# Router and feed-forward part of a sandwich layer: float32r halves replaced by fp16 halves scaled by powers of two

## The chip, the cores and the metric

One NeuronCore of a Trainium2 chip runs the whole program. The metric is the device time of one execution in microseconds (us); three runs of the kernel before are known, and one further execution was profiled.

## The reference, cut to what matters

```python
x = x + ln(attention(ln(x)))     # 2048 tokens of 256, 16 heads of 128
x = x + ln(ffn(ln(x)))

def ffn(x):                      # 8 experts, inner width 176, top 2
    probs = softmax(x @ Wr)      # router, [256, 8]
    w, i  = top_k(probs, 2);  w = w / sum(w)
    g = einsum('bsh,ehi->besi', x, Wg)
    u = einsum('bsh,ehi->besi', x, Wu)
    y = einsum('besi,eih->besh', silu(g) * u, Wd)
    return sum over e of combine[e] * y[e]
```

Weights, inputs and result are float32. The attention weights come as fp4 codes with block scales. `ln` is a layer norm without gain and bias, so it gives the same result for any power of two that multiplies its input, if its epsilon is multiplied by the square of that power.

## The kernel before, in words

The kernel reaches float32 accuracy by splitting each operand into a high and a low half and doing three products: high by high, high by low, low by high. In attention both halves are fp16 (HP); in the router and the feed-forward part both halves are float32r. Everything is recorded under a manual schedule, so the order of instructions on each engine is the order of the Python calls, and each engine works through its own list in order.

**Attention** is a loop of 258 steps `g` (L676), 16 heads of 16 query tiles (`h, t = divmod(g, 16)`). A step does on TensorE twelve 512-column matmuls of scores (`scores_half`, L447, two halves of six) and twelve of probabilities times values (`pv_unit`, L517 to L519, two units of six) for tiles further back. VectorE takes the maxima of both halves (L458), the negated maximum (L462), the inverse of the sum (L476, L479) and the low half of the probabilities (`pl`, L498, two pieces). ScalarE does two exponentials (L469) and the high half (`ph`, L483). SP then transposes `ph` and `pl` by DMA (L486, L502) into `pt`. Scores are in three PSUM buffers, `pl` in two of SBUF, `ph` in three.

`fill(h, t)` (L538) adds projections for later heads to a step: a query or key projection (four matmuls of 512 columns, L191) in even `t`, a value projection (four of 256, L216) in odd `t` of an odd head. Its PSUM tile has the tag `pj`, of which there is one; ScalarE copies it out (L204, L235) after the exponentials of that step, and GpSimd splits it. In even heads `load_w` brings the next head pair's codes and scales through GpSimd's DMA queue (L130, L135) at `t` = 0, 3 and 6, 512 KB each time. Every fourth step GpSimd writes 256 KB of attention output to memory (`ot_d`, L533).

**The last head** (`late`, L647) also loads the rest of the output weights and the gate weights `wg`, and splits these in four pieces (`split_piece`, L602: a high copy on ScalarE, a subtraction on GpSimd). The up weights `uw` and down weights `dw` are split after attention, before the feed-forward loop.

**The router** transposes a normed block of 512 tokens (`tr`, L808), splits it, and multiplies it by `rw` (L833); its logits go through a top-2 on VectorE, and the combine weights through memory (`ct_d`), from where they are broadcast as `cu`.

**The feed-forward loop** (L1112) has four blocks of 512 tokens by eleven chunks of 128 inner columns, 44 chunks in all. `gate_up` (L906) does 12 matmuls of 512 columns (L914); ScalarE takes the sigmoid (L934), VectorE three products (L935, L936, L939), ScalarE the high half of the hidden value and GpSimd its low half (L927, L928). `down` (L943), two chunks behind, does 12 matmuls of 256 columns (L953). Between the chunks lie the output projection of later blocks (L759, fp16 by bf16), the norms on VectorE, and the router of the next block.

Of the kernel before, what the change touches and what calls it, by code (L numbers as in the profile page):

```python
# [8 lines left out]
F32 = mybir.dt.float32  # L9
# [21 lines left out]
ISQ = 1.0 / 128.0 ** 0.5  # L31
XS = 1024.0
PS = 16384.0
POOL_COLS = 512


@with_exitstack
def sandwich(
# [35 lines left out]
    ssc = const.tile([128, 2], F32)  # L74
    sgv = const.tile([128, 1], F32)

    def rstd_of(mv, n, pool):
        v = pool.tile([128, n], F32, name="ln_v")
        nc.vector.tensor_scalar(v, mv[:, :, 1], EPS, None, ALU.add)
# [7 lines left out]
    one3 = const.tile([3, 128], F32)  # L87
    bvT = bT[:, 2]
    bv3 = const.tile([128, NH, 3], BF)
    crow = const.tile([128, D], F32)  # L90
    rst = const.tile([128, 2, E], F32)
    rw = const.tile([128, 2, 2, E], F32R)
    res = const.tile([128, 2, NH], F32)

    def tail_consts(i):
        if i == 0:
            nc.sync.dma_start(out=crow, in_=bo.partition_broadcast(128))
            nc.sync.dma_start(out=rst, in_=wr.rearrange("(kc p) e -> p kc e", p=128))
            nc.gpsimd.iota(iota8, [[1, 8]], base=0, channel_multiplier=0,
                           allow_small_or_imprecise_dtypes=True)  # L100
        else:
            nc.gpsimd.tensor_copy(bv3[:, :, 0], bvT)
            nc.gpsimd.tensor_tensor(res[:, 0], bvT, bv3[:, :, 0], ALU.subtract)
            nc.gpsimd.tensor_copy(bv3[:, :, 1], res[:, 0])
            nc.gpsimd.tensor_tensor(res[:, 1], res[:, 0], bv3[:, :, 1], ALU.subtract)
            nc.gpsimd.tensor_copy(bv3[:, :, 2], res[:, 1])
            nc.gpsimd.tensor_copy(rw[:, 0], rst)
            nc.gpsimd.tensor_tensor(rw[:, 1], rst, rw[:, 0].bitcast(F32), ALU.subtract)

    small = ctx.enter_context(tc.tile_pool(name="small", bufs=4))  # L110
    proj_ctx = ExitStack()
# [127 lines left out]
    with tc.tile_pool(name="start", bufs=4) as st:  # L239
# [18 lines left out]
        for i, (which, codes, scales) in enumerate(  # L258
# [8 lines left out]
        nc.gpsimd.memset(one3, 1.0)  # L267

        make_identity(nc, ident)
        def scale_bcast(which, ps):  # L270
# [32 lines left out]
        def sig_pow():  # L303
            nc.vector.tensor_reduce(t3[:, 0:1], sgp["t"][:3, :128], AX.X, ALU.max)
            nc.vector.tensor_scalar(t3[:, 1:2], t3[:, 0:1], 1e-30, None, ALU.max)
            nc.vector.tensor_scalar(
                t3.bitcast(I32)[:, 2:3], t3.bitcast(I32)[:, 1:2], 0x7F800000, None,
                ALU.bitwise_and,
            )
            nc.vector.tensor_scalar(t3[:, 3:6], ident[:3, :3], t3[:, 2:3], None, ALU.mult)  # L310
            ps = psA.tile([128, 512], F32, name="sgb", tag="pj")
            nc.tensor.matmul(ps[:, :3], one3, t3[:, 3:6], start=True, stop=True)
            sgp["s"] = ps

        def sig_all():
# [280 lines left out]

    def bias_row2(b3):
        pb2 = psA.tile([128, 512], F32, name="pb2", tag="pj")
        nc.tensor.matmul(pb2[:, :D], one3, b3, start=True, stop=True)
        nc.vector.tensor_tensor(crow, pb2[:, :D], crow, ALU.add)  # L600

    def split_piece(dst, stg, on_pool):  # L602
        nc.scalar.copy(dst[0], stg)
        eng = nc.gpsimd if on_pool else nc.vector
        eng.tensor_tensor(dst[1], stg, dst[0].bitcast(F32), ALU.subtract)

    gu_raw = {}

# [6 lines left out]
        )  # L615
        return stg

    def split_gu(dst, i, stg, on_pool):
        kc, eh = divmod(i, 2)
        cs = slice(4 * I * eh, 4 * I * eh + 4 * I)  # L620
        split_piece(
            (dst[:, 0, kc, cs], dst[:, 1, kc, cs]),
            stg.rearrange("p e i -> p (e i)"), on_pool,
        )

    OIN = {}
# [20 lines left out]
    def late(t):  # L647
        nonlocal gw
        if t in WO_LOAD:
            load_wo(3 + WO_LOAD.index(t), kqv, ("kT", "kT"), 8)  # L650
        if t - 1 in WO_LOAD:
            dequant_wo(3 + WO_LOAD.index(t - 1))
        if t == 13:
            bias_row2(gst.pop("b3"))
        if t == 12:
            gst["b3"] = bias_row()
        if t == 9:
            proj_ctx.close()
            rp = ctx.enter_context(tc.tile_pool(name="gw", bufs=1, side="right"))
            gw = rp.tile([128, 2, 2, EI], F32R)  # L660
        if 10 <= t < 14:
            split_gu(gw, t - 10, gst.pop(t - 10), True)
# [13 lines left out]
    for g in range(NS + 2):  # L676
# [123 lines left out]
    def ln_b2(b):  # L800
        MV2[b] = small.tile([128, 4, 2], F32, name="mv2")
        stats(X1[b], MV2[b], 0, 4)
        R2[b] = rstd_of(MV2[b], 4, small)

    def ln_c(b):
        norm(AT[b], X1[b], MV2[b], R2[b])

    def tr(b, kc, tag="pj"):  # L808
        xn = AT[b]
        if kc == 0 and b == 0:  # L810
            XT[b] = [
                kqv.tile([128, 2, 512], F32R, name="xT0", tag="v", bufs=7)
                for _ in range(2)
            ]
        elif kc == 0:
            xt = tl.tile([128, 2, 2, 512], F32R, name="xT", bufs=2)
            XT[b] = [xt[:, 0], xt[:, 1]]
        xh, xl = XT[b]
        ps = aux_psum([128, 512], F32, "trp", tag)
        for t in range(4):  # L820
            nc.tensor.transpose(ps[:, bass.ts(t, 128)], xn[:, t, bass.ts(kc, 128)], ident)
        nc.scalar.copy(xh[:, kc], ps)
        nc.vector.tensor_tensor(xl[:, kc], ps, xh[:, kc].bitcast(F32), ALU.subtract)

    LGT, LG, CW = {}, {}, {}

    def router_a(b, tag="pj"):
        xT = XT[b]
        ps = aux_psum([8, 512], F32, "rp", tag)
        n = 0  # L830
        for kc in range(2):
            for a, w in ((0, 0), (1, 0), (0, 1)):
                nc.tensor.matmul(  # L833
                    ps, rw[:, w, kc, :], xT[a][:, kc, :], start=(n == 0), stop=(n == 5)
                )
# [43 lines left out]
    def router_d(b):  # L879
        cw = CW.pop(b)  # L880
        pc = psA.tile([E, 512], F32, name="pct", tag="pj")
        for t in range(4):
            nc.tensor.transpose(pc[:, bass.ts(t, 128)], cw[:, 0, t, :], ident)
        ct = small.tile([E, 512], F32, name="cT", bufs=1)
        nc.scalar.copy(ct, pc)
        nc.sync.dma_start(out=ct_d[b], in_=ct)

    CU = {}
# [17 lines left out]
    def gate_up(b, c):  # L906
# [11 lines left out]
                    n += 1  # L918
        sg = tl.tile([128, 512], F32, name="sg", bufs=3)
        cu = CU.pop((b, c))  # L920
        hh = tl.tile([128, 2, 512], F32R, name="hh", bufs=3)
        ends = b == 3 and c >= NCH - 2
        parts = 2 if b == 3 and c == NCH - 1 else 1

        def low(f):
            fs = bass.ts(f, 512 // parts)
            nc.scalar.copy(hh[:, 0, fs], sg[:, fs])  # L927
            (nc.vector if ends else nc.gpsimd).tensor_tensor(  # L928
                hh[:, 1, fs], sg[:, fs], hh[:, 0, fs].bitcast(F32), ALU.subtract
            )  # L930

        for f in range(parts):
            fs = bass.ts(f, 512 // parts)
            nc.scalar.activation(sg[:, fs], ps[:, 0, fs], AF.Sigmoid)  # L934
# [33 lines left out]
    def fin1(b):  # L968
        MV3[b] = small.tile([128, 4, 2], F32, name="mv3")
        stats(YT[b], MV3[b], 0, 4)  # L970
        R3[b] = rstd_of(MV3[b], 4, small)

    def fin2(b):
        y = YT[b]
# [10 lines left out]
    def fin_last(b):  # L985
# [189 lines left out]
```

## Time and profile before

| What | us |
|---|---|
| median of three runs | 1884.12 (1881.57 to 1884.13) |
| the profiled execution, its own time | 1879.05 |
| its span, first to last instruction | 1877.3 |
| attention loop, first to last score maximum (L458) | 31.3 to 1582.0 |
| an odd head without weight loads (1, 3, 5, 7, 9, 11, 13), each | 94.3 |
| even heads 2, 4, 6, 8, 10, 12 | 98.1, 97.7, 99.7, 99.0, 97.1, 100.8 |
| first feed-forward chunk to the last (L914) | about 1641 to 1865 |

A head is taken from the L462 of its first step to that of the next head. The profile lists, by line, engine and operation, how often an instruction ran and how long one took. The mean duration of a TensorE matmul is longer than the distance between two starts, since consecutive ones overlap; for matmuls the distance of starts in the timeline is the cost. "Idle before" names what ended the waiting of an engine.

### The profile page before, as it was taken

Reading aid. Unit: us, or ns where it says so; the run is one execution under the profiler, and the core shown is the slowest. Engines: PE = TensorE matmul, PEld = TensorE weight load, DVE = VectorE, ACT = ScalarE, POOL = GpSimd, SP = SyncE. Lnnn points to the kernel's source line nnn. Section 1 sums busy time; section 2 is a strip of 40 time slices with the busy share of each in tenths; the row PEclk is TensorE's granted clock in tenths of the full one; section 3 lists DMA queues with packets and bytes.
Section 4 is the critical chain, followed back from the end, with each engine's and each line's share of the span. In section 5 each row is a group of like instructions: output and inputs, shape, how many; then the busy total and the mean of one; then the engine's idle time right before and its main releaser. Section 6 shows DMA issues by size and latency. Waiting matters only on the chain. (4 is left out here: it accounts for less than half of the span.)

```text
span 1877.3 us, 25533 instructions
## 1 busy us (share of the span) xinstructions
PE 1794.1 (96%) x8890; PEld 936.0 (50%) x8890; DVE 1632.4 (87%) x2267; ACT 1365.5 (73%) x1730; POOL 907.5 (48%) x893
## 2 busy tenths in 40 slices
PE   7899999999999999999999999999999988899998
PEld 4344444444444444444444444444444434588887
DVE  7999989998999899998999999889999886458566
ACT  5888878888888788887888888778888776123232
POOL 3554574457544654465445644564444342233222
PEclk9999999999999999999999999999999999999999
DMA  3999999999999999999999999999999999982121
GB/s 91 190 193 190 189 202 198 190 189 202 196 191 189 193 195 191 192 201 193 188 190 205 197 189 192 183 202 194 191 186 205 208 220 219 259 236 69 55 71 57
DMA packets 1133345, 342.31 MB, mean 182 GB/s; under 512 B 1070896, under 2 KB 1120768, under 8 KB 1133216
## 3 DMA queue, kind: packets, MB, share of 16 engines
q1 hardware_dynamic: 1120528, 310.53, 90.4%
q0 software_dynamic: 9584, 27.82, 5.9%
q10 hardware_dynamic: 3104, 2.33, 0.5%
q8 instruction: 70, 1.15, 0.2%
q14 instruction: 59, 0.48, 0.1%
HBM read 53.22 MB, written 18.94 MB: 38 GB/s over the span
## 5 line engine op out<-in xcount | busy, mean ns | idle before, releaser
L498 DVE SCALAR_TENSOR_TENSOR pl<-p,m,ph 128x1024 f16<-128x1024 f32 x512 | 731.6, 1429 | 50.2 <-DMA pt<-pl 43.9
L469 ACT ACTIVATE p<-s,m,ssc 128x1024 f32<-128x1024 f32 x512 | 611.9, 1199 | 192.6 <-DVE m L462 158.9
L458 DVE TENSOR_REDUCE m<-s 128x1 f32<-128x1024 f32 x512 | 622.0, 1215 | 23.2 <-PE s L457 22.7
L483 ACT ACTIVATE ph<-p,m 128x2048 f16<-128x2048 f32 x256 | 513.0, 2004 | 84.7 <-issue 30.2
L518 PE MATMUL pv<-pt,v 128*128 128x512 f16 x1024 | 391.2, 382 | 27.9 <-DMA pt<-pl 27.9
L453 PE MATMUL s<-kT,qT 128*128 128x512 f16 x1024 | 389.9, 381 | 16.9 <-ACT p L469 13.9
L517 PE MATMUL pv<-pt,v 128*128 128x512 f16 x1024 | 390.6, 381 | 7.4 <-DMA pt<-ph 5.3
L519 PE MATMUL pv<-pt,v 128*128 128x512 f16 x1024 | 391.2, 382 | 0.0
L454 PE MATMUL s<-kT,qT 128*128 128x512 f16 x1024 | 389.8, 381 | 0.0
L457 PE MATMUL s<-kT,qT 128*128 128x512 f16 x1024 | 305.3, 380 | 0.0
L205 POOL CAST qT<-t 128x512 f16<-128x512 f32 x63 | 86.4, 1371 | 247.2 <-ACT t L204 247.2
L236 POOL CAST v<-t 128x256 f16<-128x256 f32 (+1 forms) x105 | 54.3, 517 | 271.8 <-ACT t L235 271.8
L518 PEld LDWEIGHTS <-v 128*128 128x128 f16 x1024 | 100.7, 98 | 153.8 <-issue 29.4
L454 PEld LDWEIGHTS <-qT 128*128 128x128 f16 x1024 | 100.4, 98 | 135.2 <-issue 33.4
L517 PEld LDWEIGHTS <-v 128*128 128x128 f16 x1024 | 100.6, 98 | 130.8 <-issue 7.0
L519 PEld LDWEIGHTS <-v 128*128 128x128 f16 x1024 | 100.7, 98 | 123.6 <-issue 7.6
L457 PEld LDWEIGHTS <-qT 128*128 128x128 f16 x1024 | 100.5, 98 | 121.8 <-issue 1.7
L453 PEld LDWEIGHTS <-qT 128*128 128x128 f16 x1024 | 100.6, 98 | 111.3 <-issue 3.2
L237 POOL TENSOR_TENSOR v<-t,v 128x256 f16<-128x256 f32 (+1 forms) x105 | 146.8, 1398 | 8.4
L928 POOL TENSOR_TENSOR hh<-sg,hh 128x512 fp32r<-128x512 f32 x42 | 54.5, 1298 | 144.6 <-ACT hh L927 99.4
L927 ACT CAST hh<-sg 128x512 fp32r<-128x512 f32 (+1 forms) x45 | 27.5, 611 | 118.4 <-DVE sg L939 118.4
L206 POOL TENSOR_TENSOR kT<-t,kT 128x512 f16<-128x512 f32 x60 | 107.8, 1796 | 5.0
(184 smaller groups left out, 2019.4 us busy)
## 6 DMA issues: line engine op xcount, KB each, us to landing
oi<-ot_d SPq DMA_DIRECT2D x32, 512.0 KB, 6.9
ot_d<-o POOLq DMA_DIRECT2D x63, 256.0 KB, 4.1
pt<-ph SPq DMA_TRANSPOSE x256, 5.1
pt<-pl SPq DMA_TRANSPOSE x256, 4.7
cu<-ct_d SPq DMA_DIRECT2D x16, 256.0 KB, 3.9
xt<-in_L_attn_x SPq DMA_DIRECT2D x4, 512.0 KB, 5.6
wos<-in_L_attn_wo_scales ACTq DMA_DIRECT2D x32, 64.0 KB, 4.5
woc<-in_L_attn_wo_codes SPq DMA_DIRECT2D x8, 256.0 KB, 3.5
```

The costliest lines, as they stand in the source:

```text
L206: nc.gpsimd.tensor_tensor(t[:, 1, :], t32, t[:, 0, :], ALU.subtract)
L237: nc.gpsimd.tensor_tensor(v[:, 1, sl, :], t32, v[:, 0, sl, :], ALU.subtract)
L453: nc.tensor.matmul(s[:, j, :], q[:, 0, qc], k[:, 0, :], start=True, stop=False)
L454: nc.tensor.matmul(s[:, j, :], q[:, 0, qc], k[:, 1, :], start=False, stop=False)
L457: nc.tensor.matmul(s[:, j, :], q[:, 1, qc], k[:, 0, :], start=False, stop=True)
L458: nc.vector.tensor_reduce(m[:, half : half + 1], s, AX.XY, ALU.max)
L469: nc.scalar.activation(p[:, bass.ts(i, 1024)], s, AF.Exp, bias=m[:, 2:3], scale=ssc[:, 0:1], accum_out=m[:, 3 + i : 4 + i],)
L483: nc.scalar.activation(ph, p, AF.Copy, scale=m[:, 6:7])
L498: nc.vector.scalar_tensor_tensor(pl[:, cs], p[:, cs], m[:, 6:7], ph[:, cs], ALU.mult, ALU.subtract)
L517: nc.tensor.matmul(ps, vh, d[:, :, c, :], start=(c == 0), stop=False)
L518: nc.tensor.matmul(ps, vh, d[:, :, 16 + c, :], start=False, stop=False)
L519: nc.tensor.matmul(ps, vl, d[:, :, c, :], start=False, stop=(c == 15))
```

## The change

Router and feed-forward operands (`rw`, the normed input `xT`, `gw`, `uw`, `dw`, the hidden value `hh`) become pairs of fp16 in place of float32r. To keep fp16 in range, each weight is multiplied by 1024 divided by the power of two of its largest entry. These four maxima are found by the kernel:

- `max_load` and `max_piece`: the three expert weights (1.44 MB each) are read a second time, in 24 pieces of 128x352 (180 KB) through GpSimd's DMA queue, one every second step of heads 3, 4 and 5; VectorE reduces each piece three steps later, in odd `t`, with one further small reduction after every eighth.
- `wscale`: in head 7, after steps 3, 5 and 7, three stages bring the maxima across partitions (a TensorE transpose, a small matmul that broadcasts, 15 small VectorE instructions) and split `rw`.
- `split_piece` gets one more ScalarE pass over each of the eleven staged weight pieces; the subtraction stays on GpSimd.
- The sigmoid, the logits' copy and the combine weights' copy take a scale in the ScalarE instruction that they had; the norms take a scaled epsilon.

```diff
-    rw = const.tile([128, 2, 2, E], F32R)
+    rw = const.tile([128, 2, 2, E], HP)
...
-            nc.gpsimd.tensor_copy(rw[:, 0], rst)
-            nc.gpsimd.tensor_tensor(rw[:, 1], rst, rw[:, 0].bitcast(F32), ALU.subtract)
+    def max_load(i, j):
+        src = (wg, wu, wd)[i].rearrange("e a b -> (e a b)").rearrange("(p n) -> p n", p=128)
+        wms[(i, j)] = stage.tile([128, 352], F32, name="wmx", bufs=2)
+        nc.gpsimd.dma_start(out=wms[(i, j)], in_=src[:, bass.ts(j, 352)])
+    def max_piece(i, j):
+        if j == 0:
+            wms[i] = small.tile([128, 8], F32, name="wms", bufs=1)
+        nc.vector.tensor_reduce(
+            wms[i][:, j : j + 1], wms.pop((i, j)), AX.X, ALU.max,
+            apply_absolute_value=True,
+        )
+        if j == 7:
+            nc.vector.tensor_reduce(wm[:, i : i + 1], wms.pop(i), AX.X, ALU.max)
+    def wscale(i):
+        if i == 0:
+            nc.vector.tensor_reduce(
+                wm[:, 3:4], rst, AX.XY, ALU.max, apply_absolute_value=True
+            )
+            ps = psA.tile([128, 512], F32, name="wmt", tag="pj")
+            nc.tensor.transpose(ps[:4, :128], wm, ident)
+            w4 = small.tile([4, 8], F32, name="w4", bufs=1)
+            nc.vector.tensor_reduce(w4[:, 0:1], ps[:4, :128], AX.X, ALU.max)
+            wms["w4"] = w4
+        elif i == 1:
+            w4 = wms.pop("w4")
+            nc.vector.tensor_scalar(w4[:, 1:2], w4[:, 0:1], 1e-30, None, ALU.max)
+            nc.vector.tensor_scalar(
+                w4.bitcast(I32)[:, 2:3], w4.bitcast(I32)[:, 1:2], 0x7F800000, None,
+                ALU.bitwise_and,
+            )
+            nc.vector.tensor_scalar(w4[:, 4:8], ident[:4, :4], w4[:, 2:3], None, ALU.mult)
+            ps = psA.tile([128, 512], F32, name="wmb", tag="pj")
+            nc.tensor.matmul(ps[:, :4], one4, w4[:, 4:8], start=True, stop=True)
+            nc.vector.tensor_copy(swt[:, 0], ps[:, :4])
+        else:
+            nc.vector.reciprocal(swt[:, 3], swt[:, 0])
...
+            nc.vector.tensor_scalar(sr, rst, swt[:, 1, 3:4], None, ALU.mult)
+            nc.vector.tensor_copy(rw[:, 0], sr)
+            nc.vector.tensor_tensor(rw[:, 1], sr, rw[:, 0], ALU.subtract)
...
-    def split_piece(dst, stg, on_pool):
+    def split_piece(dst, stg, i):
+        nc.scalar.activation(stg, stg, AF.Copy, scale=swt[:, 1, i : i + 1])
         nc.scalar.copy(dst[0], stg)
-        eng = nc.gpsimd if on_pool else nc.vector
-        eng.tensor_tensor(dst[1], stg, dst[0].bitcast(F32), ALU.subtract)
+        nc.gpsimd.tensor_tensor(dst[1], stg, dst[0], ALU.subtract)
...
-            gw = rp.tile([128, 2, 2, EI], F32R)
+            gw = rp.tile([128, 2, 2, EI], HP)
...
+        if t % 2 == 0 and 48 <= g < 96:
+            max_load(*divmod(g // 2 - 24, 8))
+        if t % 2 == 1 and 51 <= g < 99:
+            max_piece(*divmod(g // 2 - 25, 8))
+        if h == 7 and t in (3, 5, 7):
+            wscale((t - 3) // 2)
...
-        nc.scalar.copy(LGT[b], ps)
+        nc.scalar.activation(LGT[b], ps, AF.Copy, scale=swt[:8, 2, 3:4])
...
-        hh = tl.tile([128, 2, 512], F32R, name="hh", bufs=3)
+        hh = tl.tile([128, 2, 512], HP, name="hh", bufs=3)
...
-            nc.scalar.activation(sg[:, fs], ps[:, 0, fs], AF.Sigmoid)
+            nc.scalar.activation(sg[:, fs], ps[:, 0, fs], AF.Sigmoid, scale=swt[:, 2, 0:1])
...
-    uw = uwp.tile([128, 2, 2, EI], F32R)
+    uw = uwp.tile([128, 2, 2, EI], HP)
...
-    dw = tl.tile([128, 2, NCH, D], F32R)
+    dw = tl.tile([128, 2, NCH, D], HP)
```

The three calls in the attention loop stand at the end of a step, after `fill`. `XN` (64) scales the normed input and `HC` (2 to the power -35) the combine weights.

More of the change, by code (lines that the diff above doesn't have):

```diff
@@ L33 @@
 PS = 16384.0
-POOL_COLS = 512
+XN = 64.0
+HC = 2.0 ** -35
 @with_exitstack
@@ L75, in sandwich, with rstd_of @@
     sgv = const.tile([128, 1], F32)
-    def rstd_of(mv, n, pool):
+    def rstd_of(mv, n, pool, eps=EPS, mul=1.0):
         v = pool.tile([128, n], F32, name="ln_v")
-        nc.vector.tensor_scalar(v, mv[:, :, 1], EPS, None, ALU.add)
+        nc.vector.tensor_scalar(v, mv[:, :, 1], eps, mul, ALU.add, ALU.mult)
         r = pool.tile([128, n], F32, name="ln_r")
@@ L86, in sandwich @@
     iota8 = const.tile([128, 8], F32)
-    one3 = const.tile([3, 128], F32)
+    one4 = const.tile([4, 128], F32)
     bvT = bT[:, 2]
@@ L91, in sandwich @@
     rst = const.tile([128, 2, E], F32)
-    rw = const.tile([128, 2, 2, E], F32R)
+    rw = const.tile([128, 2, 2, E], HP)
+    wm = const.tile([128, 4], F32)
+    swt = const.tile([128, 4, 4], F32)
+    epc = const.tile([128, 2], F32)
     res = const.tile([128, 2, NH], F32)
@@ new lines, in sandwich @@
+    wms = {}
+    def wscale(i):
[21 more added lines that the diff above has]
+            nc.vector.reciprocal(swt[:, 3], swt[:, 0])
+            nc.vector.tensor_scalar(swt[:, 1], swt[:, 3], XS, None, ALU.mult)
+            nc.vector.tensor_scalar(swt[:, 2], swt[:, 0], 1.0 / (XS * XN), None, ALU.mult)
+            nc.vector.tensor_scalar(
+                epc[:, 0:1], swt[:, 3, 0:1], swt[:, 3, 1:2], 128.0, ALU.mult, ALU.mult
+            )
+            nc.vector.tensor_scalar(epc[:, 0:1], epc[:, 0:1], swt[:, 3, 2:3], None, ALU.mult)
+            nc.vector.tensor_scalar(
+                epc[:, 1:2], epc[:, 0:1], epc[:, 0:1], EPS, ALU.mult, ALU.mult
+            )
+            sr = small.tile([128, 2, E], F32, name="sr", bufs=1)
+            nc.vector.tensor_scalar(sr, rst, swt[:, 1, 3:4], None, ALU.mult)
+            nc.vector.tensor_copy(rw[:, 0], sr)
+            nc.vector.tensor_tensor(rw[:, 1], sr, rw[:, 0], ALU.subtract)
@@ L266, in sandwich @@
             cds[which] = (i, cd)
-        nc.gpsimd.memset(one3, 1.0)
+        nc.gpsimd.memset(one4, 1.0)
         make_identity(nc, ident)
@@ L311, in sig_pow @@
             ps = psA.tile([128, 512], F32, name="sgb", tag="pj")
-            nc.tensor.matmul(ps[:, :3], one3, t3[:, 3:6], start=True, stop=True)
+            nc.tensor.matmul(ps[:, :3], one4[:3], t3[:, 3:6], start=True, stop=True)
             sgp["s"] = ps
@@ L598, in bias_row2 @@
         pb2 = psA.tile([128, 512], F32, name="pb2", tag="pj")
-        nc.tensor.matmul(pb2[:, :D], one3, b3, start=True, stop=True)
+        nc.tensor.matmul(pb2[:, :D], one4[:3], b3, start=True, stop=True)
         nc.vector.tensor_tensor(crow, pb2[:, :D], crow, ALU.add)
-    def split_piece(dst, stg, on_pool):
+    def split_piece(dst, stg, i):
+        nc.scalar.activation(stg, stg, AF.Copy, scale=swt[:, 1, i : i + 1])
         nc.scalar.copy(dst[0], stg)
-        eng = nc.gpsimd if on_pool else nc.vector
-        eng.tensor_tensor(dst[1], stg, dst[0].bitcast(F32), ALU.subtract)
+        nc.gpsimd.tensor_tensor(dst[1], stg, dst[0], ALU.subtract)
     gu_raw = {}
@@ L616, in load_gu, with split_gu @@
         return stg
-    def split_gu(dst, i, stg, on_pool):
+    def split_gu(dst, i, stg, which):
         kc, eh = divmod(i, 2)
@@ L622, in split_gu @@
             (dst[:, 0, kc, cs], dst[:, 1, kc, cs]),
-            stg.rearrange("p e i -> p (e i)"), on_pool,
+            stg.rearrange("p e i -> p (e i)"), which,
         )
@@ L659, in late @@
             rp = ctx.enter_context(tc.tile_pool(name="gw", bufs=1, side="right"))
-            gw = rp.tile([128, 2, 2, EI], F32R)
+            gw = rp.tile([128, 2, 2, EI], HP)
         if 10 <= t < 14:
-            split_gu(gw, t - 10, gst.pop(t - 10), True)
+            split_gu(gw, t - 10, gst.pop(t - 10), 0)
         if t in WG_LOAD:
@@ L802, in ln_b2 @@
         stats(X1[b], MV2[b], 0, 4)
-        R2[b] = rstd_of(MV2[b], 4, small)
+        R2[b] = rstd_of(MV2[b], 4, small, mul=1.0 / (XN * XN))
     def ln_c(b):
@@ L809, in tr @@
         xn = AT[b]
[L810 to L816, printed above, removed]
+        if kc == 0:
+            if b == 0:
+                xt = kqv.tile([128, 2, 2, 512], HP, name="xT0", tag="v", bufs=7)
+            else:
+                xt = tl.tile([128, 2, 2, 512], HP, name="xT", bufs=2)
             XT[b] = [xt[:, 0], xt[:, 1]]
@@ L822, in tr @@
         nc.scalar.copy(xh[:, kc], ps)
-        nc.vector.tensor_tensor(xl[:, kc], ps, xh[:, kc].bitcast(F32), ALU.subtract)
+        nc.vector.tensor_tensor(xl[:, kc], ps, xh[:, kc], ALU.subtract)
     LGT, LG, CW = {}, {}, {}
@@ L884, in router_d @@
         ct = small.tile([E, 512], F32, name="cT", bufs=1)
-        nc.scalar.copy(ct, pc)
+        nc.scalar.activation(ct, pc, AF.Copy, scale=HC)
         nc.sync.dma_start(out=ct_d[b], in_=ct)
@@ L928, in low @@
             (nc.vector if ends else nc.gpsimd).tensor_tensor(
-                hh[:, 1, fs], sg[:, fs], hh[:, 0, fs].bitcast(F32), ALU.subtract
+                hh[:, 1, fs], sg[:, fs], hh[:, 0, fs], ALU.subtract
             )
@@ L970, in fin1 @@
         stats(YT[b], MV3[b], 0, 4)
-        R3[b] = rstd_of(MV3[b], 4, small)
+        R3[b] = rstd_of(MV3[b], 4, small, epc[:, 1:2])
     def fin2(b):
@@ L991, in fin_last @@
             stats(dps, mv, t0, t0 + 2)
-            r.append(rstd_of(mv[:, t0 : t0 + 2], 2, small))
+            r.append(rstd_of(mv[:, t0 : t0 + 2], 2, small, epc[:, 1:2]))
         nb = small.tile([128, 2], F32, name="nb", bufs=1)
@@ L1034, in sandwich @@
     for i in range(2):
-        split_gu(uw, i, ust[i], True)
+        split_gu(uw, i, ust[i], 1)
         ust.append(load_gu(wu, i + 2, uwp, "raw", 2))
@@ L1046, in sandwich @@
     for i in range(2, 4):
-        split_gu(uw, i, ust[i], True)
+        split_gu(uw, i, ust[i], 1)
     pt_ctx.close()
     tl = ctx.enter_context(tc.tile_pool(name="tl", bufs=1, reuse_waits="tile"))
-    dw = tl.tile([128, 2, NCH, D], F32R)
+    dw = tl.tile([128, 2, NCH, D], HP)
     dsrc = wd.rearrange("e i d -> (e i) d").rearrange("(c p) d -> p c d", p=128)
@@ L1059, in split_d @@
     def split_d(stg, c0, c1):
-        split_piece((dw[:, 0, c0:c1], dw[:, 1, c0:c1]), stg[:, : c1 - c0], True)
+        split_piece((dw[:, 0, c0:c1], dw[:, 1, c0:c1]), stg[:, : c1 - c0], 2)
     def load_x1(b):
```

## Prediction

> **What bounds the kernel now.** I read the busy times and the slices first.
>
> ```profile
> PE 1794.1 (96%) x8890; PEld 936.0 (50%) x8890; DVE 1632.4 (87%) x2267; ACT 1365.5 (73%) x1730; POOL 907.5 (48%) x893
> ...
> PE   7899999999999999999999999999999988899998
> ...
> DVE  7999989998999899998999999889999886458566
> ```
>
> TensorE is full nearly everywhere, VectorE with it until slice 32 (1550 us), only TensorE from slice 35 on. So attention and feed-forward are two questions. For attention, the busy times of heads 3, 4 and 5, where the maxima are to be taken:
>
> ```profile
> 325.10:419.40 94.30, 94.11 (x452) 44.00 (x450) 90.38 (x112) 79.80 (x100) 45.99 (x46) 1.00 1.05 188
> 419.40:517.10 97.70, 93.98 (x448) 43.37 (x447) 89.06 (x113) 80.22 (x99) 61.96 (x62) 1.00 1.12 201
> 517.10:611.40 94.30, 94.10 (x451) 44.00 (x450) 90.38 (x112) 79.80 (x100) 46.00 (x46) 1.00 1.07 190
> ```
>
> The columns are length, PE, PEld, DVE, ACT, POOL, clock, DMA share, GB/s. An odd head always takes 94.3; an even one does the same arithmetic but carries 1.5 MB of weight loads, and takes 97.1 to 100.8. VectorE idles 3.9 of 94.3. What ends its waits in an odd head (head 7):
>
> ```profile
> DVE m L476 <- ACT p L469: 2.3, 8, 0.3
> ```
>
> It waits 0.28 us for the exponential in every second step, never for TensorE: a VectorE/ScalarE loop runs level with TensorE. For feed-forward, the chain that ended last:
>
> ```profile
> 1695.87 0.61 ACT sg L934
> ...
> 1720.06 0.66 PE trp L821 x4
> ...
> 1742.18 2.75 PE gup L914 x12
> 1744.93 1.43 PE dps L953 x12
> ...
> 1751.00 7.00 PE op L759 x64
> ```
>
> From 1666 to 1865 it is TensorE end to end, except 1696 to 1720 and 1765 to 1785, where VectorE works without a gap on norms and products.
>
> **Feed-forward matmuls (gain).** Now 2.75/12 = 229 ns for 512 columns and 1.43/12 = 119 ns for 256. fp16 stands in the same trace: ten score and value matmuls of 512 columns start 2.16 us apart (216 ns), and L759 gives 7.00/64 = 109 ns for 256 columns with fp16 weights. A chunk saves 12 x 13.5 + 12 x 10 = 0.28 us. [...] But fp16 streams of this trace hold 216 ns for 1500 us, so I take 216. Of the 44 chunks, one before 1661, 4.7 in 1666 to 1696, 6.6 in 1720 to 1765 and 18.6 from 1785 on lie on TensorE's path: 31 x 0.28 = 8.7, with the router's 18 matmuls that count (231 to 216 ns) 9.0 us. The other chunks lie under the two VectorE stretches, which don't get shorter; were they on the path too the gain would be 12.8. Scales inside existing ScalarE instructions I cost at nothing: a 128x512 one with such a scale took 0.69 (L145) against 0.61 for a copy, and ScalarE waits 2 us per chunk; fp16 low halves likewise (GpSimd's 128x512 took 1.16 in fp16 at L532 and 1.30 at L928).
>
> **Maxima: VectorE (cost).** 24 reductions of 128x352. Nearest row:
>
> ```profile
> 8.68 0.55 DVE L399 TENSOR_REDUCE sm<-smax 128x3 f32<-128x384 f32 x1
> ```
>
> Less 32 columns it is 0.52, and 0.46 from start to start. It is put after `pl`'s second piece in odd `t`, ahead of the next score maximum and thus of L476, whose waits (0.28, 0.10, alternating, so 0.19 on average) it fills. Left: 0.27 each, which delays the next negated maximum, the exponentials behind it and TensorE's score buffers. Heads 3, 5 and 6 have 7 + 8 + 1 of them: 4.3 us; bounds 0 (TensorE sets the pace and hides them) and 16 x 0.46 = 7.4.
>
> **Maxima: DMA (cost).** Each piece is 180 KB on GpSimd's queue. SP's transposes occupy 77 to 80 us of an odd head and 90 to 93 of an even one: 1.5 MB of loads stretch them by 13 us, which costs the head 4.4 us on average (94.3 to 98.7). The eight new pieces of a head are 1.44 MB, but spread, each smaller than the 256 KB of `ot_d` that an odd head swallows every fourth step. In heads 3 and 5 I take 1.2 us each, for the steps where a piece meets `ot_d` (bounds 0 and 4.4). In head 4 they come on top of the loads: SP would need 93 + 13 = 106 of 97.7. I take 5, VectorE's reductions included (it waits for DMA there); bounds 2 (VectorE alone) and 11. GpSimd issues 24 more DMAs; it is busy 46 of 94, what queues behind are splits with a step of room. [...] I take no cost.
>
> Sum for the maxima: 4.3 + 2.4 + 5 = 11.7.
>
> **Scales in head 7 (cost).** Here the PSUM tag matters. The transpose after step 3 takes `pj`, the single buffer into which the step's value projection has just gone, so TensorE must wait until ScalarE has copied it out, after both exponentials:
>
> ```profile
> 727.76 0.60 PE L216 MATMUL pj<-wv,xnT 128*128 128x256 bf16 x4
> 728.20 0.38 PE L453 MATMUL s<-kT,qT 128*128 128x512 f16 x1
> 730.27 1.22 DVE L458 TENSOR_REDUCE m<-s 128x1 f32<-128x1024 f32 x1
> 731.64 0.37 ACT L235 COPY t<-pj 128x256 f32<-128x256 f32 x1
> ```
>
> TensorE now goes on at 728.20. With the transpose it stands until 732.05, takes 0.3, and starts the scores at 732.4: 4.2 later. Behind it VectorE's next maximum waits for six score matmuls (1.46): 733.8 instead of 730.27, 3.6 later. TensorE is busy 94.11 of 94.30 in such a head, so nothing is won back: 3.8. The second stage, after step 5, meets the same buffer (its projection ends at 739.9, its copy at 743.4): 3.8 again. The third is nine dependent VectorE instructions at 0.19 (L316 to L318): 1.7, less 0.2 of idle, 1.5. Sum 9.1; bounds 4 (each stage only its own work and a semaphore) and 11.
>
> **Splits (cost).** Eleven more ScalarE passes: 0.77 for 704 columns, 1.05 for 1024. In the last head ScalarE waits for `ph` or the maximum after three of four pieces; 0.5 us. After attention:
>
> ```profile
> 1642.82 1.05 ACT L603 CAST dw<-draw 128x1024 fp32r<-128x1024 f32 x1 [5.02 <-DMA draw<-in_L_ffn_Wd]
> ...
> 1643.95 2.41 POOL L605 TENSOR_TENSOR dw<-draw,dw 128x1024 fp32r<-128x1024 f32 x1 [3.72 <-ACT dw L603]
> ```
>
> Behind this subtraction GpSimd has the norm's power (L81), for which VectorE and then the second chunk wait: plus 1.05, less 0.25 for fp16. Earlier the second `uw` pair holds ScalarE from 1629.6 to 1632.5, so the combine weights' copy at 1632.23 slips 0.3. The staging tiles of `uw` get other addresses, and SP's first load of them now waits for transposes too, up to 2 us with output loads behind; these have some 8 us of room, so I take 0.9 of it. Sum 2.5; bounds 0.5 and 5. Two `rw` instructions leave GpSimd: nothing.
>
> **Sum.** 11.7 + 9.1 + 2.5 - 9.0 = +14.3. On the profiled execution's own 1879.05 (span 1877.3 and 1.75 around it) that is 1893.4, 0.76% more. The median of the runs shown, 1884.12, lies 5.1 above it; the same share gives 1898.5.
>
> **Rivals.**
>
> *DMA becomes the bound of heads 3 to 5.* The DMA share is 1.05 already, and a 512 KB burst lengthens steps from 5.8 to 7.5. Then heads 3 and 5 pay 4.4 + 2.2 each and head 4 pays 11: 24.2 in place of 11.7, 1911. Against it: `ot_d` bursts cost odd heads nothing.
>
> *The additions fall into idle time, and the kernel is faster.* One mechanism: attention's waits (L476, SP's 16 idle us per odd head) take in all the reductions and loads, and the two round trips in head 7 cost 2 each, since the engines behind the stall catch up on their own queues meanwhile. Attention then pays 4, splits 1.5, and feed-forward gains 12: 1884.1 - 6.5 = 1877.6. It decides once attention's bill is under 6.5. Against it: `pj` is single, and TensorE is nearly always busy there.
>
> *Light bill:* maxima 6, scales 5, splits 2, gain 9: +4, 1888 to 1892.
>
> *fp16 brings nothing*, if the 119 and 229 ns are set by something other than the operand type: then +23, 1907. Weight loads (191 ns against 98 in fp16) point the other way.
>
> **Chances.** As summed (1892 to 1906) 0.50; DMA-bound or no fp16 gain 0.20; light 0.16; within 0.2% (3.8 us, about what a measurement can tell) 0.06; faster 0.08. So slower 0.86. The range leaves out the faster rival and the upper half of the DMA one: 1885 to 1911.
>
> **What would show it.** Heads 3 and 5 at 96 to 98, head 4 at 102 to 104, head 7 at 103; in head 7 two TensorE gaps of 4 us ahead of small matmuls in `wmt` and `wmb`; chunks of 3.9 in place of 4.18 after 1800; wmx reductions of 0.5. The forecast is wrong if head 7 stays under 98, if head 4 passes 107, or if late chunks stay at 4.18.

## The result and the profile after

The changed kernel takes 1903.4 us, the median of six runs (1899.75 to 1914.1), against 1884.03 for the kernel before beside it: a ratio of 1.0122, 95% interval 1.009 to 1.0153. Its profiled execution took 1906.36, with a span of 1904.6, 27.3 more than the span before.

From the page of the changed kernel, busy times and slices of 47.6 us:

```profile
PE 1792.9 (94%) x8893; PEld 875.9 (46%) x8893; DVE 1635.0 (86%) x2309; ACT 1379.8 (72%) x1741; POOL 904.5 (47%) x915
...
PE   7799999998999999999999999999999998889997
...
PEclk9999999998999999999999999999999999999999
```

PEld has lost 60 us, which are the shorter weight loads of fp16 (98 to 99 ns on the mean in the feed-forward loop, 191 before); PE is as busy as before. One digit is new and easy to pass over: in the tenth slice (428 to 476 us, in head 4) the granted clock is 8, under 90%. The heads that the change touches, 3, 4, 5 and 7, in the columns of the windows in the prediction:

```profile
326.00:420.80 94.80, 93.49 (x449) 43.59 (x448) 92.18 (x120) 80.27 (x101) 49.77 (x53) 1.00 1.09 203
422.20:531.60 109.40, 98.69 (x449) 44.71 (x448) 90.23 (x122) 80.23 (x99) 62.92 (x70) 0.94 1.06 195
531.60:626.40 94.80, 94.24 (x452) 43.97 (x451) 92.31 (x121) 80.28 (x100) 50.39 (x54) 1.00 1.08 201
727.20:834.30 107.10, 99.44 (x453) 45.16 (x452) 91.89 (x127) 79.93 (x100) 43.47 (x46) 0.95 0.94 167
```

Heads 3 and 5 are hardly longer than the 94.3 of before, with eight and nine more VectorE instructions. Heads 4 and 7 are 12 and 13 us longer, and they alone have a clock of 0.94 and 0.95. From the chain that ended last, two chunks near the end:

```profile
1860.40 2.59 PE gup L974 x12
1864.30 2.59 PE gup L974 x12
```

They start 3.90 us apart, where it was 4.18, and twelve matmuls take 2.59 in place of 2.75.

Where the span went, cut at the negated maximum of each head's first step and at the first and last sigmoid:

| Part | before | after | more | predicted |
|---|---|---|---|---|
| heads 3 and 5 | 188.6 | 189.4 | +0.7 | +6.7 |
| head 4 | 97.7 | 109.4 | +11.7 | +5 |
| head 7 | 94.3 | 107.1 | +12.8 | +9.1 |
| heads 0, 2, 6, 8, 10, 12, 14 | 689.3 | 697.8 | +8.5 | 0 |
| start, heads 1, 9, 11, 13 | 412.7 | 412.5 | -0.2 | 0 |
| head 15 to the first sigmoid | 161.2 | 161.8 | +0.6 | +2.5 |
| first sigmoid to the last | 222.7 | 213.7 | -9.0 | -9.0 |
| last sigmoid to the end | 10.8 | 12.9 | +2.1 | 0 |
| span | 1877.3 | 1904.6 | +27.3 | +14.3 |

(One of the predicted reductions, 0.3 us, lies in head 6 and is counted with heads 3 and 5.) The two profiled executions differ by 8 us more than the medians do, and the fourth row, where the change adds nothing, is of that size: over the thirteen kernels profiled here, its seven even heads add up to anything from 685 to 699 us (697 in e1, which has neither maxima nor scales). I don't read it as an effect of the change.

The last row is one. GpSimd's longest DRAIN instruction, at the end of the program, grew by as much. Before and after (shortest, median and longest of three, in ns):

```profile
L1171 POOLq DRAIN  x3: 46/102/4987, 1871.5 to 1877.0; - x3
L1231 POOLq DRAIN  x3: 46/102/6948, 1896.8 to 1904.3; - x3
```

It takes 6.95 us in all eight kernels profiled here that issue the 24 loads on GpSimd's queue, 4.99 in those without them (before, e1, e11) and in e10, which issues them on SP's queue, and 5.07 in e6, which has one. That is 0.08 us for each further DMA on GpSimd's queue.

### The profile page after: what moved, and what is told of

The parts are those of the page before. It is cut to its first block, busy times and chain, and to the rows that moved or that the text cites. A ratio compares the mean times of both kernels' runs of the same rounds, so it can differ in the third digit from the quotient of the medians.

```text
span 1904.6 us, 25635 instructions
## 1 busy us (share of the span) xinstructions
PE 1792.9 (94%) x8893; PEld 875.9 (46%) x8893; DVE 1635.0 (86%) x2309; ACT 1379.8 (72%) x1741; POOL 904.5 (47%) x915
## 5 line engine op out<-in xcount | busy, mean ns | idle before, releaser
L575 PEld LDWEIGHTS <-v 128*128 128x128 f16 x1024 | 101.2, 99 | 123.5 <-issue 8.3
L988 POOL TENSOR_TENSOR hh<-sg,hh 128x512 f16<-128x512 f32 x42 | 49.0, 1166 | 141.2 <-ACT hh L987 99.9
L987 ACT CAST hh<-sg 128x512 f16<-128x512 f32 (+1 forms) x45 | 27.4, 608 | 116.4 <-DVE sg L999 116.4
L262 POOL TENSOR_TENSOR kT<-t,kT 128x512 f16<-128x512 f32 x60 | 102.2, 1703 | 5.0
```

The source lines that it names most:

```text
L262: nc.gpsimd.tensor_tensor(t[:, 1, :], t32, t[:, 0, :], ALU.subtract)
L575: nc.tensor.matmul(ps, vl, d[:, :, c, :], start=False, stop=(c == 15))
```

## Experiments

All eleven are edits of the changed kernel. The times of a group (e1 to e4, e5 to e8, e9 to e11) come from one chip and stand beside runs of the kernel before on it; ratios are compared across groups. In each profile the heads that matter are:

| Kernel | head 3 | head 4 | head 5 | head 7 | ratio to before, 95% interval |
|---|---|---|---|---|---|
| before | 94.3 | 97.7 | 94.3 | 94.3 | 1 |
| the change | 94.5 | 109.4 | 94.8 | 107.1 | 1.0122 (1.009 to 1.0153) |
| e1 fp16 alone | 94.4 | 99.9 | 94.4 | 95.4 | 0.9965 (0.9944 to 0.9986) |
| e2 loads in odd heads | 94.4 | 99.3 | 94.4 | 94.4, head 9 106.0 | 1.0066 (1.0043 to 1.0088) |
| e3 scales moved | 94.4 | 107.5 | 98.4 | 94.3 | 1.0054 (1.003 to 1.0078) |
| e4 both moves | 94.4 | 101.2 | 96.4 | 94.7 | 1.002 (1.0005 to 1.0035) |
| e5 loads alone | 96.3 | 105.9 | 94.5 | 95.3 | 1.0035 (1.0014 to 1.0056) |
| e6 reductions alone | 94.4 | 98.6 | 94.6 | 95.3 | 0.9963 (0.9946 to 0.9979) |
| e7 stops filled | 94.4 | 109.6 | 95.3 | 102.1 | 1.0088 (1.0055 to 1.012) |
| e8 odd heads, no scales | 95.4 | 103.3 | 94.5 | 96.1 | 0.9992 (0.997 to 1.0013) |
| e9 spread | 94.1 | 100.7 | 93.9 | 94.0 | 0.9975 (0.9955 to 0.9995) |
| e10 SP's queue | 94.4 | 101.7 | 95.6 | 94.4 | 0.9983 (0.9956 to 1.0011) |
| e11 scales alone | 94.4 | 100.4 | 94.4 | 94.4 | 0.9946 (0.9927 to 0.9966) |

**The theory** after the result: fp16 gains what was forecast, and the whole loss is in two places, the loads of head 4 (transfers, not VectorE) and the two stops of TensorE in head 7, made dearer by a slower TensorE clock behind each stop (0.51 and 0.50 in the windows behind them). **Rivals**: the cost of maxima and scales is spread over all of attention, and moving them saves little; VectorE's reductions are what head 4 pays for; the stop alone is the price in head 7.

### e1: fp16 alone

No loads, no reductions, and constants in place of the scales' first two stages, so the factors are not taken from the weights; the third stage stays.

```diff
-        if t % 2 == 0 and 48 <= g < 96:
-            max_load(*divmod(g // 2 - 24, 8))
-        if t % 2 == 1 and 51 <= g < 99:
-            max_piece(*divmod(g // 2 - 25, 8))
-        if h == 7 and t in (3, 5, 7):
-            wscale((t - 3) // 2)
+        if h == 7 and t == 3:
+            nc.gpsimd.memset(swt[:, 0, 0:3], 0.25)
+            nc.gpsimd.memset(swt[:, 0, 3:4], 0.125)
+        if h == 7 and t == 7:
+            wscale(2)
```

> The changed kernel without the search for maxima: no extra loads, no reductions, no stages across partitions; the four powers of two are constants (0.25 three times, 0.125) that GpSimd writes in head 7, and only the third stage of VectorE instructions stays there. Theory A (the cost sits in head 4 and head 7 alone, the feed-forward part gives 9 us less 2 to 3 for splits, and the differences of the other even heads in the two profiles are scatter): all odd heads at 94.3 to 96, head 4 at about 98, 1877 us, 7 below the kernel before. Theory B (the change also slows other even heads, 0, 6, 8 and 10 by 8.6 us together, through the new placement of tiles): 1885, level with the kernel before, with those heads still at 100 to 103.

1880.99 us, 0.35% or 6.6 us less than before. The gain is there (-9.0 and the splits' 2.5 would make 6.5). Between its two theories e1 does not decide: the time lies midway between 1877 and 1885, and heads 6, 8 and 10 are at 100.4 to 101.8, as theory B said. The kernel before has one profile to compare even heads with, so a cost of a few us there is not ruled out. The rest of the change costs (1.0122 - 0.9965) x 1884 = 30 us. Head 7 keeps 1.0 for the third stage.

### e2, e3, e4: move the loads, move the scales, move both

e2 takes the eight pieces of each weight in heads 3, 5 and 7, which carry no other loads (scales in head 9):

```diff
-        if t % 2 == 0 and 48 <= g < 96:
-            max_load(*divmod(g // 2 - 24, 8))
+        if h in (3, 5, 7) and t % 2 == 0:
+            max_load(h // 2 - 1, t // 2)
...
```

> The 24 loads and reductions in heads 3, 5 and 7, which have no weight loads, in place of 3, 4 and 5; the three scale stages move from head 7 to head 9, unchanged. Theory A (loads cost only where they meet the weight loads of an even head): head 4 back to about 98, heads 3, 5 and 7 at 94.3 to 95, head 9 at about 107; 1892, some 11 below the changed kernel. Rival (the DMA queue is so full that the pieces cost 4 us or more in any head): heads 3, 5, 7 at 98 or more, 1898 to 1904.

e3 leaves the loads and cuts the scales into four stages at ends of steps where `pj` has no value projection waiting for ScalarE:

```diff
-        if h == 7 and t in (3, 5, 7):
-            wscale((t - 3) // 2)
+        if (h, t) == (8, 0):
+            wscale(0)
+        if (h, t) == (8, 1):
+            wscale(1)
+        if (h, t) == (10, 1):
+            wscale(2)
+        if (h, t) == (10, 11):
+            wscale(3)
...
```

> Loads and reductions as in the changed kernel; the scale stages cut in four and put at the ends of steps 0 and 1 of head 8 and 1 and 11 of head 10. Step 1 of an even head has no projection, so the transpose and the small matmul find their PSUM buffer free and their operands ready. Theory A (head 7 pays for two stops of TensorE and for half speed after them, 12.8 us in all): head 7 at 94.3, heads 8 and 10 under 1 us more than in the kernel before, 1891. Rival (the small instructions themselves and the passage between engines cost most of it, wherever they stand): heads 8 and 10 together 8 or more us longer, 1899 or above.

e4 does both, with the stages in heads 10 and 12.

> Both moves together: loads and reductions in heads 3, 5 and 7, scale stages in steps 0 and 1 of head 10 and 1 and 11 of head 12. Theory A: 11.7 and 12.8 us of the changed kernel are gone, what stays is the feed-forward gain less splits: 1879 (1876 to 1882), faster than the kernel before by 0.2 to 0.4%. Theory B (scattered costs in other heads belong to the change): 1886 to 1890.

Measured 1899.05, 1893.94 and 1889.15 us. In ratios, e2 saves 0.0056 (10.6 us) and e3 0.0068 (12.8), so each place is worth about what its head shows (each difference is known to some 7 us), and most of the bill is not spread over attention. e2's head 4 is back at 99.3 and its odd heads at 94.4, and its head 9 pays 11.7 as head 7 did; e3's head 7 is back at 94.3. But e2 missed theory A's 1892 and falls in the rival's 1898 to 1904 although its heads speak for A. e4 missed theory A's 1876 to 1882 too and ended in B's 1886 to 1890 (1889.15); it keeps 0.0055, 10 us, above e1. Moving the loads does not make them free.

### e5, e6: loads without reductions, reductions without loads

e5 leaves out `max_piece`; e6 reduces one loaded piece 24 times. Both have constants in the first two stages, so neither takes its factors from the weights.

```diff
+        if g == 46:
+            max_load(0, 0)
+            wms["one"] = wms.pop((0, 0))
         if t % 2 == 1 and 51 <= g < 99:
-            max_piece(*divmod(g // 2 - 25, 8))
+            i, j = divmod(g // 2 - 25, 8)
+            wms[(i, j)] = wms["one"]
+            max_piece(i, j)
...
```

> Leaves out the reductions of the maxima and stages 1 and 2 of the scales (constants in their place, so the factors are not taken from the weights); the 24 loads of 180 KB stay in heads 3, 4 and 5. Theory A (head 4's 11.7 us come from transfers in flight beside the two DMA transposes of each step and the next heads' weight loads): head 4 stays at 105 to 110 us, heads 3 and 5 at 94.3, head 7 at 95; the time is that of the kernel with constant factors (0.9965) plus 6 to 10 us, 1.000 to 1.002. Rival B (the reductions on VectorE make head 4 late): head 4 at 97 to 101, the time 0.996 to 0.998.

> The counterpart: all 24 reductions run, but each on the same one piece that was loaded once, so no other loads are there, and stages 1 and 2 are constants as before. Theory A (transfers): head 4 at 97 to 101, as without any maxima; the time 0.996 to 0.998. Rival B (reductions): head 4 at 105 to 110, the time 1.000 to 1.002. If both this and the run with the loads alone show 97 to 101, it takes the two together.

e5 1892.5 us, e6 1879.78. The reductions cost nothing, not even in head 4 (98.6), and e6's ratio is that of e1; the loads bring head 4 to 105.9, and the two kernels lie 0.0072 or 13.6 us apart, more than theory A gave. With e3's 0.0068 for the scales that makes 0.0140 of the 0.0157 between the change and e1. What head 4 waits for in e6 (us in all, times, longest):

```profile
DVE pl L554 <- DMA pt<-pl: 4.1, 2, 3.8
...
DVE m L514 <- PE s L513: 2.8, 6, 0.9
```

Before it was this:

```profile
DVE pl L498 <- DMA pt<-pl: 3.3, 4, 1.8
```

The same view of the changed kernel:

```profile
DVE pl L554 <- DMA pt<-pl: 9.0, 3, 5.8
DVE m L514 <- PE s L513: 8.5, 8, 3.0
...
PE pv L574 <- DMA pt<-pl: 5.9, 3, 2.8
PE pv L573 <- DMA pt<-ph: 4.8, 1, 4.8
```

The wait that grew is that for the transposes, in which VectorE wants a free `pl` and TensorE its `pt`. SP's queue in the worst step of the changed kernel (12.4 us, from 452.6):

```profile
443.28 2.71 SPq L542 DMA_TRANSPOSE pt<-ph  x1
446.08 5.81 SPq L558 DMA_TRANSPOSE pt<-pl  x1
451.98 6.11 SPq L542 DMA_TRANSPOSE pt<-ph  x1
458.19 3.02 SPq L558 DMA_TRANSPOSE pt<-pl  x1
```

Two transposes in a row take 5.8 and 6.1, while the weight loads of the next heads and a `wmx` piece are in flight. In odd heads without loads the median is 2.2; with weight loads alone, single ones of 4.6 to 5.7 us are common (20 in heads 2 to 12 before), and the longest pair of head 4 before is 9.9. Over all of head 4 a transpose takes 2.8 to 2.9 us on the mean in the nine profiles without extra loads there and 3.0 to 3.2 in the four with them. What follows on TensorE, in windows:

```profile
454.00:460.00 6.00, 3.03 (x15) 1.18 (x12) 1.31 (x1) 2.25 (x6) 2.98 (x4) 1.00 1.23 174
460.00:468.00 8.00, 3.84 (x9) 1.27 (x10) 6.62 (x9) 4.62 (x6) 6.04 (x8) 0.52 1.16 188
```

PE is busy for 6.9 of the 14 us from 454 to 468, and behind the stop the granted clock is 0.52 (third from the right).

### e7: the stops of head 7 filled with matmuls that are thrown away

`warm` issues so many score matmuls into the score buffer of the next step, where the real ones write over them.

```diff
+        if h == 7 and t in (3, 5):
+            warm(h, t + 1, 18 if t == 3 else 14)
         if h == 7 and t in (3, 5, 7):
             wscale((t - 3) // 2)
...
```

> The changed kernel, with 18 and 14 score matmuls that are thrown away put on TensorE just ahead of the two small products of head 7, so that TensorE works through 3.9 and 3.0 us in which it stood still. Nothing that it waits for comes earlier. Theory A (after the stops TensorE runs at half clock: 13 matmuls of 0.427 in place of 0.216 us behind the first, 9 behind the second, 2.8 + 1.9 us): no spacing of 0.43 is left in head 7, and head 7 falls from 107.1 to 102.4; the time falls by 4 to 5 us, from 1.0122 to about 1.0097. Rival B (the cost is the stop alone, and VectorE and ScalarE set the pace behind it whatever TensorE's clock): head 7 stays at 106.5 to 107.5.

First the stop in the changed kernel, on TensorE:

```profile
743.65 0.60 PE L272 MATMUL pj<-wv,xnT 128*128 128x256 bf16 x4
748.14 0.37 PE L135 MATMUL wmt<-ident,wm 128*4 128x128 f32 x1 [3.90 <-ACT t L291]
748.32 0.63 PE L509 MATMUL s<-kT,qT 128*128 128x512 f16 x1
748.74 0.63 PE L510 MATMUL s<-kT,qT 128*128 128x512 f16 x1
...
753.86 0.40 PE L510 MATMUL s<-kT,qT 128*128 128x512 f16 x1
754.10 0.38 PE L509 MATMUL s<-kT,qT 128*128 128x512 f16 x1
```

The wait is the predicted one, ScalarE's copy of the value projection (L291) out of `pj`. What was not predicted is that the scores behind it start 0.427 us apart until 753.9, and only then 0.216 again. The same place in e7:

```profile
741.37 0.60 PE L272 MATMUL pj<-wv,xnT 128*128 128x256 bf16 x4
741.81 4.05 PE L508 MATMUL s<-kT,qT 128*128 128x512 f16 x18
745.70 0.27 PE L135 MATMUL wmt<-ident,wm 128*4 128x128 f32 x1
745.80 0.38 PE L520 MATMUL s<-kT,qT 128*128 128x512 f16 x1
746.02 0.38 PE L521 MATMUL s<-kT,qT 128*128 128x512 f16 x1
```

From the projection to `wmt` it is as long (4.33 against 4.49), since the same copy is waited for, but the scores behind it go at 0.216. The granted clock is halved nowhere in this head 7, and the head takes 102.1: 5.0 less, 4.7 expected. The steps of `t` = 3 and 5 fall from 11.45 and 10.52 to 8.91 and 8.88. The whole kernel's 1899.27 us (1.0088) moves the way theory A says, though its interval alone would not carry it; the head does.

### e8 and e11: what the moved version keeps

e8 has e2's loads and reductions and e1's constants; e11 has the four stages in heads 10 and 12, and constants for the three expert weights' maxima. Neither takes the expert weights' factors from the weights.

> Loads and reductions in heads 3, 5 and 7, stages 1 and 2 of the scales left out (constants), stage 3 kept. It splits what the version with both moves costs above the version without maxima (1.0020 against 0.9965, 10 us). Theory A (loads and reductions are free in odd heads; the rest is in the stages of the scales and scatter of the even heads): odd heads 94.4, the time 0.996 to 0.998. Rival B (loads in odd heads still cost, in the even heads that follow or in the tail): 1.000 to 1.002.

> No loads and no reductions (the weights' three maxima are given as constants, so the factors are not taken from the weights); the stages of the scales run at the free places in heads 10 and 12. Theory A (the loads in odd heads keep a few us): the stages cost the 1.0 us of their last step and little else, the time 0.996 to 0.998. Rival B (the stages are what the version with both moves kept): 0.999 to 1.002.

e8 1885.24, e11 1876.19. e11 at 0.9946 is not above e1: stages at free places cost nothing that can be measured. e8 at 0.9992 lies between its two theories, 0.0046 (9 us) above e11, so more than half of what e4 kept is in the loads; the 0.0028 between e8 and e4 is within their intervals. Three parts of it show:

- The longer DRAIN at the end takes 2.0 us.
- Of the 20 odd heads with eight loads in the profiles of the change, e2 to e5, e7, e8 and e10, eleven are within 0.25 of 94.3, but single steps of 7.4 to 10 us make others up to 4.1 longer; the mean is 0.7, some 2 us for three heads.
- Every run's granted clock is on record, and (1 - clock) times the span is the most that a halved clock can take away. On the mean of the runs it is 22.4 us in e11, 25.0 in e8 and 26.2 in e4.

The rest stays open, since the even heads scatter by more.

### e9 and e10: a better place for the loads

e9 is the whole change with four or five pieces a head in heads 1, 3, 5, 7, 9 (every third step), stages as in e4; e10 is e4 with `nc.sync` in place of `nc.gpsimd` for the pieces.

```diff
+        if h in (1, 3, 5, 7, 9) and t % 3 == 0 and t < 15 and 5 * (h // 2) + t // 3 < 24:
+            max_load(*divmod(5 * (h // 2) + t // 3, 8))
...
```

> The whole change, with the loads five to a head (every third step) in heads 1, 3, 5, 7 and 9, where they were eight in heads 3, 5 and 7, and the stages of the scales at the ends of steps where the projections' PSUM tile is free, in heads 10 and 12. Theory A (what the version with both moves kept above the one without maxima comes from loads that follow each other closely): odd heads 94.4, the time 0.997 to 0.9995. Rival B (each load costs the same wherever it is, or the stages are what costs): as before, 1.001 to 1.003.

> The version with both moves (loads in heads 3, 5, 7; stages in heads 10 and 12), its 24 loads issued on SP's queue behind the transposes, in place of GpSimd's. Theory A (loads cost because they run at the same time as the transposes, wherever they are issued): odd heads 94.4 to 95.5, the time as with GpSimd's queue, 1.000 to 1.004. Rival B (the queue: GpSimd's own work or its descriptors delay what follows): the time falls to 0.997 to 0.9995. A third outcome, transposes stuck behind a load in SP's queue, would show heads 3, 5 and 7 at 97 or more.

e9 1883.37 us, 0.9975 (0.9955 to 0.9995): the whole function, and faster than both kernels, by 4.7 and some 28 us. Its five odd heads with loads are at 94.1 or below, and the time is in theory A's range. That the spacing does it is not shown, though: e8 and e10, with eight loads to a head, are at 0.9992 and 0.9983, and their intervals overlap with e9's.

e10 is in rival B's range, but its interval reaches 1.0011 and e4's begins at 1.0005. So what the queue costs is shown for the 2.0 us of the DRAIN, which e10 does not pay, and not settled beyond. The third outcome is ruled out: heads 3, 5 and 7 are at 94.4, 95.6 and 94.4.

## Why the prediction was right, and where its steps were not

The forecast of 1898.5 in 1885 to 1911 held the time, and most of the loss came from the two places where it was put, heads 4 and 7. But the increase was forecast as 0.76% and measured as 1.22%. That the sum came this near is partly luck: the reductions and the loads of heads 3 and 5 were put too high, head 4 and head 7 too low, and one cost was put at nothing.

- **Feed-forward, -9.0: right in mechanism, near in size.** The matmuls run at 2.59/12 = 216 ns, as the trace's own fp16 rows said. First to last sigmoid is 222.7 before and 213.7 after, but that the two numbers agree to the tenth is chance. The first sigmoid ran 0.1 us behind its matmuls before, and runs 2.2 behind them now (they end at 1675.8), with a split and its extra pass (L659) ahead of it:

```profile
1675.83 1.15 ACT L659 ACTIVATE draw<-draw,swt 128x1024 f32<-128x1024 f32 x1 [3.64 <-DMA draw<-in_L_ffn_Wd]
1677.01 1.04 ACT L660 CAST dw<-draw 128x1024 f16<-128x1024 f32 x1
1677.96 0.68 ACT L994 ACTIVATE sg<-gup,swt 128x512 f32<-128x512 f32 x1
```

  From the first matmul on the gain is 7.1, of which the last 17 chunk intervals give 4.5. The two stretches of VectorE hardly got shorter, as forecast: 27.6 to 27.1 us from chunk 9 to 15, 24.0 to 23.6 from 22 to 27. In the other eleven profiles of fp16, first to last sigmoid takes 213.5 to 215.5.
- **Reductions on VectorE, 4.3: wrong.** The failed step is "waits (0.28, 0.10, alternating, so 0.19 on average) it fills. Left: 0.27 each". A step of head 3 without a reduction and one with it, in the changed kernel:

```profile
376.26 1.22 DVE L514 TENSOR_REDUCE m<-s 128x1 f32<-128x1024 f32 x1
377.76 0.21 DVE L532 TENSOR_SCALAR m<-m 128x1 f32<-128x1 f32 x1 [0.28 <-ACT p L525]
...
382.07 0.51 DVE L120 TENSOR_REDUCE wms<-wmx 128x1 f32<-128x352 f32 x1
382.50 1.21 DVE L514 TENSOR_REDUCE m<-s 128x1 f32<-128x1024 f32 x1
383.63 0.20 DVE L532 TENSOR_SCALAR m<-m 128x1 f32<-128x1 f32 x1
```

  The reduction takes 0.43 from start to start, as forecast, and the wait of 0.28 behind it is gone. Of the 0.15 left over 0.02 or 0.03 shows, since TensorE sets the pace (94.1 of 94.3 busy) and finds its scores taken in time: such steps last 5.84 or 5.85 in place of 5.82. e6 puts the bill of all 24 at nothing that can be measured. The forecast's own lower bound, "TensorE sets the pace and hides them", was the truth; it had used the same 94.11 of 94.30 for head 7 and not here.
- **Loads in heads 3 and 5, 2.4: too high for the heads.** Both together cost 0.7 with the reductions here, and one 0.7 on the mean of all profiles. A transpose takes 2.7 us on the mean in these heads, where it was 2.4 and 2.5; 32 of them are 88 us, for which 94 have room. At the level of the whole kernel, loads in odd heads cost 14 us in e4 and 5 in e9 (against e11, each give or take 5).
- **Head 4, 5 us with bounds 2 and 11: the mechanism was right, the size short.** The profiled pair gives 11.7, but before's 97.7 is the lightest head 4 of the nine profiles without loads in it (97.7 to 103.3, mean 100.3). The four with loads have 105.9 to 109.6, mean 108.1. So the mean price is 7.8. By the forecast's own sign, "if head 4 passes 107", this part of it was wrong. One term was missing: behind the stop the clock is at 0.50, while TensorE has 9.8 us of work (6.4 from 460.4 to 470.6, 3.4 from 518.4 to 521.8), so up to 4.9 us go there. No run takes this apart in head 4, and even heads without the loads have such stretches too.
- **Scales in head 7, 9.1 with bounds 4 and 11: right in mechanism, too small.** Measured 12.8, as 5.6 and 0.7 in the steps of `t` = 3 and 4, 4.7 in that of 5, 1.8 in that of 7. Stops of 3.90 and 3.03 stand where 4.2 and 4.2 were put. The sum left out the halved clock behind them, 5.0 by e7; without it, 102.1 - 94.3 = 7.8, less than forecast.
- **GpSimd's queue, "I take no cost": wrong by 2.0.** The loads were issued in 0.54 to 0.59 us each and landed in time (in 8.4 us at most, where three steps are 17), but 24 more of them make the DRAIN at the end longer, 6.95 in place of 4.99.
- **Splits, 2.5:** head 15 to the first sigmoid grew by 0.6. No run takes them alone, and this stretch scatters too (161.2 to 163.8 in the twelve profiles that have them, mean 162.5, against the one 161.1 before), so 2.5 is neither shown nor ruled out.
- **The rivals.** DMA as the bound of heads 3 to 5 (1911): true of head 4 (7.8 us), not of the odd heads (0.7). The additions falling into idle time: true of all reductions, and of the stages once they are moved; a kernel faster than before comes out of it in e9. The light bill (+4 us, a ratio of 1.002) is ruled out by the interval, which begins at 1.009. fp16 bringing nothing is ruled out by e1.

## What to carry to other kernels

A second pass over data for a small statistic was cheap here in heads without other loads (0.7 us a head, by the heads' own times) and dear where its transfers met others (7.8 in head 4), so place its loads by what else is in flight, not by VectorE's idle time. Ahead of any new TensorE instruction ask which PSUM buffer it takes and who still has to empty that; the same stages cost 12.8 us behind value projections and nothing measurable where the buffer was free. In this kernel a stop of TensorE of over 2 us cost its length and mostly, by my estimate, another 1.7 us for each 3.4 us of halved clock behind it (half of it, as far as TensorE has work), so read the clock of the window that follows, not only the idle time. Look at the end of the program too: the queue that a load is issued on had a price there (2.0 us for 24 loads).

## What the runs showed of the hardware that was not expected

Behind most stops of over 2 us TensorE ran at half speed for a while, at a granted clock of 0.50. In the changed kernel's head 7, windows ahead of and behind the two stops (clock third from the right):

```profile
743.00:748.00 5.00, 1.25 (x8) 0.59 (x6) 3.49 (x5) 4.11 (x6) 1.83 (x1) 0.91 1.14 214
748.00:754.00 6.00, 5.86 (x15) 2.14 (x16) 2.97 (x5) 1.35 (x2) 1.06 (x2) 0.51 0.53 95
754.00:762.00 8.00, 8.00 (x39) 3.60 (x37) 6.04 (x8) 5.55 (x7) 2.00 (x2) 1.00 0.70 131
```

And in e7, over the place of the first:

```profile
746.00:752.00 6.00, 6.00 (x29) 2.74 (x28) 4.91 (x8) 2.44 (x2) 0.61 (x1) 1.00 0.57 108
```

6 us hold 15 matmuls after the stop, 29 without it. At the halved clock matmuls of 512 columns start 0.427 us apart, otherwise 0.216. The duration is regular too, and what sets it is not shown: in the traces of the kernel before and of the change every halved stretch (8 and 13), but for the one that the end of the program cuts off, lasts 3.41 us or a whole multiple, up to 10.24. Behind the two stops they are these:

```profile
747.07:753.90 6.83, 5.75 (x15) 2.06 (x16) 2.97 (x5) 2.18 (x4) 1.06 (x2) 0.50 0.62 112
767.55:770.97 3.42, 3.42 (x10) 1.18 (x9) 2.69 (x4) 0.54 (x2) 0.00 (x0) 0.50 0.00 0
```

TensorE is busy for 5.75 and 3.42 us in them; half of that, 4.6, is lost, and e7 got back 5.0. Stops of a little over 2 us were mostly followed by half speed too; behind this one of 2.04 it lasts until 876.8:

```profile
873.27 0.52 PE L574 MATMUL pv<-pt,v 128*128 128x512 f16 x1 [2.04 <-DMA pt<-pl]
873.58 0.63 PE L575 MATMUL pv<-pt,v 128*128 128x512 f16 x1
874.01 0.63 PE L573 MATMUL pv<-pt,v 128*128 128x512 f16 x1
```

Of 14 stops of 2 us and more in this trace (from 100 us on), 12 are followed by matmuls 0.43 us apart, 2 (2.01 and 2.13 us) are not; of 11 stops from 1.1 to 1.6 us, 4 are, two of them next to a longer one. The kernel before has such places too (at 649.6 us, after 2.02 us), in even heads, in the last head and right behind it, most of them waits for a transpose.

This goes with a good part of the scatter. Of the 74 even heads from 2 to 12 without the change's loads, 24 have no halved stretch (99.1 us on the mean), 41 have one of 3.4 us (100.3) and seven have 6.8 us (103.3). Among all 189 runs of the twelve changed kernels, a run of the same kernel that loses 1 us more by (1 - clock) times the span is 0.94 us longer (correlation 0.72). A halved clock also came behind a single stretched transpose without any load of the change in its head: one of 9.1 us in head 2 of e1 (103.9 us), one of 11.3 in head 10 of e9 (109.3). What stretches these is not shown. The 22 runs of e11 lie between 1869.3 and 1891.3, so a difference of some 8 us between two profiles of this kernel says nothing by itself.
